# A scan layer and a spectral layer on one core: z projected at its silu, a second stream of early transforms, and a reordered second block

## The chip, the core and the metric

The kernel runs on one core of a Trainium2 chip, as one program. The metric is the device time of an execution in microseconds (us). Five engines work side by side, each through its own list of instructions in order: PE (matrix products, written to PSUM), DVE, ACT and POOL (elementwise work; only DVE and ACT touch PSUM here), and SP, which here only issues DMAs. An instruction that waits holds back all that stands behind it in its engine's list.

## The reference, cut to what matters

Layer 0 takes four images x of 128 channels by 128 x 128 pixels; an image is a sequence of 16,384 steps. Matrices are applied per step; the state has 256 x 16 entries and runs along the sequence.

```
xm = relu(x @ w1 + b1) @ w2 + b2
x_in, z = split(xm @ in_proj)
u = silu(conv4(x_in) + cb)                # 4 taps along the sequence
dt, B, C = split(u @ x_proj);  delta = softplus(dt @ dt_proj + b)
h = h * exp(delta * A) + delta * B * u    # per step: 256 x 16
y = (sum_s h * C + u * D) * silu(z)
x1 = x + silu(groupnorm(y @ out_proj))
```

Layer 1 takes x1. Per image it forms four softmax weights (from a group norm, a matrix product, a relu and a mean over pixels). Per channel it takes the 2-D Fourier transform X, and with four filters W_f returns `irfft2(X * X * sum_f weight_f * W_f) + 0.5 * x1`.

## The kernel before, in words

**Block 0 (layer 0).** The sequence is cut into 128 chunks of 512 steps, 32 per image. A chunk has 16 slots; a slot n is a pair of tiles of 128 (state, channel) rows by 512 steps. The scan runs on DVE (`scans`, L396 to L420): two scan instructions per slot (L412). In even slots POOL multiplies both results by C (L419). In odd slots DVE does that itself (L414), save for one product in some chunks that changes sides. The first tile of every even slot takes its input b from PSUM: PE transposes it there (`dbu_turn`, L375 to L383, four transposes of `bt`, which ACT makes at L304). That PSUM tile exists once. The other tiles take their input from POOL (`dbu`, L363). ACT makes the factors exp(delta A) (L393). PE sums the products over states (`sums`, L422 to L435).

The order is written out by hand. `pre(k)` and `post(k)` (L184, L437) return steps as (slot, phase, function); they are laid into a table (L505 to L548) and played slot by slot. Within a slot the phases are: turn, sums, pe, exps, late, act, pool, dbu, early, gate, scans, dve, end (L550 to L554). So in PE's list the transposes that a slot's "turn" issues come ahead of that slot's sums, and these ahead of its "pe" steps. The transposes for an even slot stand at the head of the odd slot before it. `pre(k)` runs one chunk ahead of its scan. Its steps that matter here, with the slots of a chunk counted 0 to 15:

- `cv_mm(0)`, `cv_mm(1)` (L230): the convolution, eight PE passes each, in slots 0 and 1; `silu_act` (L236) on ACT in slot 2;
- `z_mm` (L219): the z projection, in slot 14; `z_act` (L225) copies it from PSUM in slot 15; `z_silu` (L241) works in place in slot 2 of the next chunk;
- the products `h1`, `xm`, `dt` and `o` share a PSUM pool with these, the pool `pp` of two banks; `turn_bank` (L178) is one more bank, used by `xd` in slot 3, by two sets of transposes in slots 5 to 14, and by some `agg` products in slot 15.

Work of layer 1 that needs x1 of earlier images is laid into chunks of later images: `finish` (L608) with its normalisation, in chunks 2 to 18 of the next image, and with its aggregation after that. `spectrum` (L468) makes the forward transform of three (or two) channel images: load in slot 4, transform over rows in 12 (PE), copy by ACT at the end of 12, transform over columns in 13 (PE), copy by ACT and store at the end of 13. One stream of these runs from chunk 52 to the end (L528 to L538), for images 0 and 1: 25 of the 64 units of block 1 are early, that is, their transforms stand ready.

**Block 1 (layer 1).** A unit is eight channels of one image (L779 to L785); it takes three steps t. It loads x1 (`xt`, six buffers) and for an early unit its transform (`sx`, two buffers) (`load`, L807). A unit that is not early is transformed by PE, with a copy by ACT and one product by DVE (L845 to L878). ACT scales the four filters (`term`, L817), POOL adds them (`mix`, L825) and forms two sums (L894); then come products on DVE, a way back through PE, copies and a store. Filters (`ft`, four buffers) are loaded four units ahead (`loads`, L795 to L800). In the first units image 3 is still normalised (32 blocks, two per three steps), and then aggregated (one block per step, t from 70); their loads are in SP's list too, three steps ahead of use. SP loads one unit ahead (L944).

## Time and profile before

| | |
|---|---|
| time, median of 3 | 7172.46 us (7171.05 to 7173.44) |
| profiled execution | 7175.45 us, its span 7173.6 us |
| block 0 | from 0 to some 6405 us |
| block 1 | from some 6425 us to the end |
| busy in the span | DVE 96%, POOL 96%, ACT 86%, PE 82% |
| scans, L412 | 3968 of 128 x 512 with a carried state, 1255 to 1268 ns each |
| a chunk of block 0 without normalisation | 48.4 and 49.1 us in turn |
| a chunk with normalisation | 50.3 us |
| mean granted PE clock | 0.897 |

A row of a group names line, engine, operation, what is written from what, and shapes; then come the count, the engine's busy time in us, the mean duration in ns, and the idle time of the engine before such instructions with what ended it. The timeline lists start and duration. A row of the waits gives total us, times and the longest. A row of a stretch gives its length, the busy time and count of each engine, the granted PE clock (PEclk, 1.00 is full speed), the DMA share and GB/s.

### The profile page before, as it was taken

What the parts mean: (1) busy time and instruction counts of PE and PEld (TensorE: products, weight loads), DVE (VectorE), ACT (ScalarE), POOL (GpSimd) and SP (SyncE); (2) the same over time, 40 slices, a digit from 0 to 9 for tenths busy, and PEclk for the clock granted to TensorE, in tenths of its full rate; (3) what the DMA queues carried; (4) which work ended last, traced back from release to release, by engine and by line L of the source; (5) the groups of instructions that cost most, each with busy time, mean ns of one, the idle gap of its engine ahead of it and who ended that gap; (6) DMA issues with size and microseconds to landing.
All of it is one profiled execution on the core that took longest, in us unless ns stands there. A gap on an engine that the chain in (4) does not pass through costs nothing.

```text
span 7173.6 us, 91384 instructions
## 1 busy us (share of the span) xinstructions
PE 5904.2 (82%) x26708; PEld 2626.8 (37%) x26708; DVE 6892.9 (96%) x7966; ACT 6143.9 (86%) x13658; POOL 6892.5 (96%) x3188
## 2 busy tenths in 40 slices
PE   6888888788787788888888788888887888867998
PEld 2333333233222233333333333333333333326888
DVE  6999999999999999999999999999999999989777
ACT  6888888888888888888888888898888888878876
POOL 6999999999999999999999999999999999988887
PEclk8888888888888889998989899999898899979999
DMA  5666666666777777777777777777777777769866
GB/s 139 160 160 152 163 159 151 165 159 165 191 176 192 179 171 176 172 184 175 189 196 186 188 176 175 178 177 184 189 191 194 177 179 177 172 164 306 236 185 162
DMA packets 905480, 1286.20 MB, mean 179 GB/s; under 512 B 81672, under 2 KB 356752, under 8 KB 904976
## 3 DMA queue, kind: packets, MB, share of 16 engines
q1 hardware_dynamic: 904832, 1280.09, 71.9%
q8 instruction: 210, 3.44, 0.2%
q14 instruction: 294, 2.41, 0.1%
q10 hardware_dynamic: 144, 0.26, 0.0%
HBM read 1023.45 MB, written 256.58 MB: 178 GB/s over the span
## 4 chain that ended last, share of the span: by engine, by line
DVE 41%; ACT 29%; issue 11%; PE 10%; DMA 5%; POOL 3%; SPq 1%; DVEq 0%; ACTq 0%; POOLq 0%
DVE da L412 20%; DVE h L412 12%; ACT da L393 12%; DVE hb L414 5%; ACT L393 3%; DMA rdelta<-dd 2%; ACT L275 2%; ACT delta L275 2%; ACT bt L304 2%; POOL hb L363 2%; DVE zs L443 1%; PE y L433 1%; POOL hb L419 1%; ACT L242 1%; DMA xt<-x 1%
## 5 line engine op out<-in xcount | busy, mean ns | idle before, releaser
L363 POOL TENSOR_TENSOR hb<-rdu,rB 128x1536 f32<-128x1536 f32 (+2 forms) x1536 | 3605.7, 2364 | 22.4 <-DMA rdelta<-dd 21.3
L393 ACT ACTIVATE da<-rdelta,amat 128x512 f32<-128x512 f32 x4096 | 2794.1, 700 | 138.3 <-DVE h L412 133.9
L419 POOL TENSOR_TENSOR hb<-h,rC 128x1024 f32<-128x1024 f32 (+1 forms) x1072 | 2435.0, 2274 | 88.8 <-DVE h L412 73.4
L412 DVE TENSOR_TENSOR_SCAN da<-da,st,hb 128x512 f32<-128x512 f32 x1976 | 2419.8, 1267 | 21.5 <-ACT da L393 14.3
L433 PE MATMUL y<-hb,sel 128*32 128x512 f32 x8192 | 1313.4, 717 | 2.9 <-POOL hb L419 2.7
L414 DVE TENSOR_TENSOR hb<-da,rC 128x512 f32<-128x512 f32 x2040 | 1296.1, 674 | 3.0
L412 DVE TENSOR_TENSOR_SCAN h<-da,st,b 128x512 f32<-128x512 f32 x992 | 1258.3, 1268 | 1.7 <-PE b L383 1.6
L412 DVE TENSOR_TENSOR_SCAN h<-da,st,hb 128x512 f32<-128x512 f32 x1000 | 1251.6, 1255 | 1.8 <-ACT da L393 1.8
L383 PE MATMUL b<-ident,bt 128*128 128x128 f32 x4096 | 748.4, 305 | 516.1 <-DVE h L412 390.6
L234 PE MATMUL pp_cv<-xm,wck 128*128 128x512 f32 x2048 | 1014.3, 640 | 1.6 <-ACT xm L217 0.8
L304 ACT ACTIVATE bt<-pt_dut,xdt 128x256 f32<-128x256 f32 x2048 | 839.4, 474 | 184.5 <-PE pt_dut L293 184.3
L383 PEld LDWEIGHTS b<-ident,bt 128*128 128x128 f32 x4096 | 531.3, 154 | 1017.1 <-DVE h L412 692.8
L415 ACT COPY st<-da 128x1 f32<-128x1 f32 x2040 | 273.1, 160 | 474.2 <-DVE hb L414 471.1
L234 PEld LDWEIGHTS pp_cv<-xm,wck 128*128 128x128 f32 x2048 | 395.9, 204 | 651.0 <-issue 422.1
L828 POOL TENSOR_TENSOR wb<-wb,term 128x1040 f32<-128x1040 f32 x192 | 461.0, 2401 | 70.8 <-ACT term L822 62.9
L293 PE MATMUL pt_dut<-ident,du 128*128 128x128 f32 x1024 | 232.4, 338 | 285.1 <-ACT xdt L286 174.9
L429 PE MATMUL y<-u,diag 128*128 128x512 f32 x512 | 303.0, 675 | 188.7 <-DVE zs L443 187.3
L293 PEld LDWEIGHTS pt_dut<-ident,du 128*128 128x128 f32 x1024 | 132.2, 162 | 604.8 <-POOL du L312 475.9
L393 ACT ACT_TABLE_LOAD x262 | 336.1, 1283 | 12.1 <-DMA rdelta<-dd 7.4
L312 POOL TENSOR_TENSOR du<-delta,u 128x512 f32<-128x512 f32 x256 | 318.8, 1267 | 25.8 <-ACT delta L275 25.8
L223 PE MATMUL pp_z<-xm,win 128*128 128x512 f32 x512 | 274.5, 634 | 51.8 <-ACT fq L497 46.2
L267 PE MATMUL pp_dt<-xd,wdt 8*128 8x512 f32 x512 | 284.8, 642 | 33.0 <-ACT pp_o L457 23.5
(160 smaller groups left out, 8139.8 us busy)
## 6 DMA issues: line engine op xcount, KB each, us to landing
rdelta<-dd SPq DMA_DIRECT2D x1024, 256.0 KB, 4.7
rdu<-dd SPq DMA_DIRECT2D x1024, 256.0 KB, 7.5
rC<-bc SPq DMA_DIRECT2D x512, 256.0 KB, 7.3
rB<-bc SPq DMA_DIRECT2D x512, 192.0 KB, 4.7
dd<-delta SPq DMA_DIRECT2D x256, 256.0 KB, 7.2
dd<-du SPq DMA_DIRECT2D x256, 256.0 KB, 5.7
ft<-in_filt_w SPq DMA_DIRECT2D x104, 520.0 KB, 7.0
ob<-o SPq DMA_DIRECT2D x128, 256.0 KB, 2.1
```

The lines of the kernel that those rows point to most:

```text
L234: nc.tensor.matmul(ps["cv", j], w, d["xm"][:, t : t + T], start=t == 0, stop=t == KC - 1)
L293: nc.tensor.transpose(ps["dut"][:, 2 * t + j, :], d["du"][:, j, at : at + P], s.ident)
L304: nc.scalar.activation(d["bt"][:, 2 * h + t, :, q, :], src, AF.Copy, scale=d["xdt"][:, 2 * h + t, R + q : R + q + 1])
L312: nc.gpsimd.tensor_tensor(du, d["delta"][:, j, :], d["u"][:, j, :], ALU.mult)
L363: nc.gpsimd.tensor_tensor(hb[:, p : p + n, :], d["du", j][:, m : m + n, :], d["B"][:, p - 1 : p - 1 + n, :], ALU.mult)
L383: nc.tensor.transpose(b[:, t * P : (t + 1) * P], src, s.ident)
L393: nc.scalar.activation(da, d["delta", j][:, m, :], AF.Exp, scale=s.amat[:, c : c + 1])
L412: nc.vector.tensor_tensor_scan(o, das[q], b, init, ALU.mult, ALU.add)
L414: nc.vector.tensor_tensor(hb[:, p + q, :], das[q], d["C"][:, p + q, :], ALU.mult)
L419: nc.gpsimd.tensor_tensor(hb[:, ps, :], h[:, q, :], d["C"][:, ps, :], ALU.mult)
L433: nc.tensor.matmul(y[m * DG : (m + 1) * DG, :], s.sel, d["hb", j, r][:, p, :], start=False, stop=r == NG - 1)
L828: nc.gpsimd.tensor_tensor(wb, wb, u[n].terms[f], ALU.add)
```

## The change

In block 0, z is no longer copied. Its first half is projected in slot 1 of the next chunk into `turn_bank`; its second half is projected from within `silu_act` in slot 2, as soon as the silu of the first convolution half has freed a bank. The silu then reads PSUM, one half at a time. The convolution moves one slot forward, to slots 15 and 0. A second stream of `spectrum` runs from chunk 84 one slot behind the first (slots 13 and 14); both take channels from the highest down. 39 units are early: all of images 0 and 1, and seven of image 2. A stream holds one SBUF tile for load, copy and store.

In block 1 the late units of image 3 stand one by one between those of images 0, 2 and 1, where before they stood in runs. A filter is kept if its next use is up to two units on. SP loads a unit two ahead, in the middle step of a unit. Units 27 to 38 are now all early; of units 42 to 60 nine are, mostly every other one. By the code the filters for units 49 and 56 are now loaded one step ahead of their use, and unit 63 loads filters once more.

```diff
-            def z_mm():
-                for j in range(NH):
-                    ps["z", j] = psum(f"z_{k}_{j}")
-                    w = s.win[:, DI + j * P : DI + (j + 1) * P]
-                    nc.tensor.matmul(ps["z", j], w, d["xm"][:, HALO:], start=True, stop=True)
-
-            def z_act():
-                d["zs"] = p2.tile([P, NH, T], F32, tag="zs", name=f"zs_{k}")
-                for j in range(NH):
-                    nc.scalar.copy(d["zs"][:, j, :], ps["z", j])
+            def z_mm(j, home):
+                ps["z", j] = home(f"z_{k}_{j}")
+                w = s.win[:, DI + j * P : DI + (j + 1) * P]
+                nc.tensor.matmul(ps["z", j], w, d["xm"][:, HALO:], start=True, stop=True)
...
                 for j in range(NH):
                     nc.scalar.activation(u[:, j, :], ps["cv", j], AF.Silu, bias=s.cb[:, j : j + 1])
+                    if j == 0 and k:
+                        st[k - 1]["z"](1, psum)
+                if k:
+                    st[k - 1]["z silu"]()
 
             def z_silu():
-                nc.scalar.activation(d["zs"], d["zs"], AF.Silu)
+                d["zs"] = p2.tile([P, NH, T], F32, tag="zs", name=f"zs_{k}")
+                for j in range(NH):
+                    nc.scalar.activation(d["zs"][:, j, :], ps["z", j], AF.Silu)
...
-                (0, "pe", partial(cv_mm, 0)), (1, "pe", partial(cv_mm, 1)), (2, "act", silu_act),
-                (NP - 2, "pe", z_mm), (NP - 1, "act", z_act), (NP + 2, "act", z_silu), (3, "pe", xd_mm), (4, "act", xd_act), (5, "pe", dt_mm), (5, "pe", xd_turn),
+                (-1, "pe", partial(cv_mm, 0)), (0, "pe", partial(cv_mm, 1)), (2, "act", silu_act),
+                (NP + 1, "pe", partial(z_mm, 0, turn_bank)), *([(NP + 2, "act", z_last)] if k == B * NCH - 1 else []), (3, "pe", xd_mm), (4, "act", xd_act), (5, "pe", dt_mm), (5, "pe", xd_turn),
...
-            return [
-                (4, "pe", load), (12, "pe", over_h), (12, "end", evict), (13, "pe", over_w), (13, "end", store),
-            ]
+            return list(zip(*zip(*slots), (load, over_h, evict, over_w, store)))
...
+        ways = [
+            ((4, "pe"), (12, "pe"), (12, "end"), (13, "pe"), (13, "end")),
+            ((5, "pe"), (13, "pe"), (13, "end"), (14, "pe"), (14, "end")),
+        ]
+        ready = [(b + 1) * NCH + NCH // 2 + 4 for b in range(B - 1)]
+        images = [(b, c0) for b in range(B - 1) for c0 in reversed(range(0, C, CC))]
+        queues = [images, [x for x in images if x[0]]]
+        free = [ready[0], ready[1]]
...
         for n, c0 in enumerate(rest):
-            units += [(c0, b) for b in (0, 2, 1, 3)]
-            for c1 in late[n * len(late) // len(rest) : (n + 1) * len(late) // len(rest)]:
-                units.append((c1, B - 1))
+            full = [(c1, B - 1) for c1 in late[n * len(late) // len(rest) : (n + 1) * len(late) // len(rest)] + [c0]]
+            for b in (0, 2, 1):
+                units += [(c0, b)] + full[:1]
+                full = full[1:]
+            units += full
...
-            ft = next((x for x in spans if x.c0 == c0 and (n - x.last == 1 or (c0 in kept and b == B - 1))), None)
+            ft = next((x for x in spans if x.c0 == c0 and (n - x.last <= 2 or (c0 in kept and b == B - 1))), None)
...
             load(0)
+            load(1)
             for t in range(3 * N + LAG + 3):
                 n, i = divmod(t, 3)
                 if i == 0:
                     for ft in loads[n]:
                         load_filter(ft)
-                    load(n + 1)
...
                 elif i == 1:
+                    load(n + 2)
                     term(n + 1, 0)
```

More of the change, by code (lines that the diff above doesn't have):

```diff
@@ L39 @@
 CC = 8
-EARLY = 2
 KEEP = 4
@@ L148 @@
     stats, outs, spectra = {}, {}, set()
-    spec = [dpool.tile([H, C, 2, WF], F32, tag=f"spec_{b}", name=f"spec_{b}") for b in range(EARLY)]
+    spec = [dpool.tile([H, C, 2, WF], F32, tag=f"spec_{b}", name=f"spec_{b}") for b in range(B - 1)]
     shared = SimpleNamespace(**{k: v for k, v in locals().items() if k not in ("ctx", "tc")})
@@ L239, in silu_act, with z_last @@
                     nc.scalar.activation(u[:, j, :], ps["cv", j], AF.Silu, bias=s.cb[:, j : j + 1])
+                    if j == 0 and k:
+                        st[k - 1]["z"](1, psum)
+                if k:
+                    st[k - 1]["z silu"]()
             def z_silu():
-                nc.scalar.activation(d["zs"], d["zs"], AF.Silu)
+                d["zs"] = p2.tile([P, NH, T], F32, tag="zs", name=f"zs_{k}")
+                for j in range(NH):
+                    nc.scalar.activation(d["zs"][:, j, :], ps["z", j], AF.Silu)
+            def z_last():
+                z_mm(1, psum)
+                z_silu()
+            d["z"], d["z silu"] = z_mm, z_silu
             def xd_mm():
@@ L466, in post, with spectrum @@
             ]
-        def spectrum(b, c0, n):
+        def spectrum(b, c0, n, way, slots):
             g = {}
             def load():
-                g["x"] = p1.tile([s.H, 3, s.W], F32, tag="fx", name=f"fx_{b}_{c0}")
-                nc.sync.dma_start(out=g["x"][:, 0:n], in_=s.x1[b][c0 : c0 + n].rearrange("c h w -> h c w"))
+                g["x"] = p1.tile([P, 3, 2 * s.WF], F32, tag=f"fs{way}", name=f"fs_{b}_{c0}")
+                nc.sync.dma_start(
+                    out=g["x"][:, 0:n, 0 : s.W], in_=s.x1[b][c0 : c0 + n].rearrange("c h w -> h c w")
+                )
@@ L476, in over_h @@
             def over_h():
-                g["pa"] = psp.tile([s.W, 3, 2 * s.WF], F32, tag="pp", name=f"pp_fa_{b}_{c0}")
+                ps = g["ps"] = psp.tile([P, 3, 2 * s.WF], F32, tag="pp", name=f"pp_fa_{b}_{c0}")
                 for q in range(n):
-                    nc.tensor.matmul(g["pa"][:, q], g["x"][:, q], s.fh, start=True, stop=True)
+                    nc.tensor.matmul(ps[:, q], g["x"][:, q, 0 : s.W], s.fh, start=True, stop=True)
             def evict():
-                g["sa"] = p1.tile([s.W, 3, 2 * s.WF], F32, tag="fs", name=f"fs_{b}_{c0}")
@@ L483, in evict @@
-                nc.scalar.copy(g["sa"][:, 0:n], g["pa"][:, 0:n])
+                nc.scalar.copy(g["x"][:, 0:n], g["ps"][:, 0:n])
             def over_w():
                 half = s.H // 2
-                g["px"] = psp.tile([s.H, 3, 2 * s.WF], F32, tag="pp", name=f"pp_fx_{b}_{c0}")
+                ps = g["ps"] = psp.tile([P, 3, 2 * s.WF], F32, tag="pp", name=f"pp_fx_{b}_{c0}")
                 for q in range(n):
-                    re, im = g["sa"][:, q, 0 : s.WF], g["sa"][:, q, s.WF :]
+                    re, im = g["x"][:, q, 0 : s.WF], g["x"][:, q, s.WF :]
@@ L490, in over_w @@
                     for (data, a, b_), start in (((re, s.fwr, s.fwr), True), ((im, s.fwi, s.fwm), False)):
                         for at, w in ((0, a), (1, b_)):
-                            o = g["px"][at * half : (at + 1) * half, q]
+                            o = ps[at * half : (at + 1) * half, q]
                             nc.tensor.matmul(o, data[:, at : at + half], w, start=start, stop=not start)
             def store():
-                x = p1.tile([s.H, 3, 2, s.WF], F32, tag="fq", name=f"fq_{b}_{c0}")
@@ L497, in store @@
-                nc.scalar.copy(x[:, 0:n].rearrange("h c r k -> h c (r k)"), g["px"][:, 0:n])
-                nc.sync.dma_start(out=s.spec[b][:, c0 : c0 + n], in_=x[:, 0:n])
-            return [
-                (4, "pe", load), (12, "pe", over_h), (12, "end", evict), (13, "pe", over_w), (13, "end", store),
-            ]
+                evict()
+                o = s.spec[b][:, c0 : c0 + n].rearrange("h c r k -> h c (r k)")
+                nc.sync.dma_start(out=o, in_=g["x"][:, 0:n])
+            return list(zip(*zip(*slots), (load, over_h, evict, over_w, store)))
@@ L527, in block0 @@
                 todo[at + (b + 1) * NCH * NP, phase].append(f)
-        chunk = NCH + NCH // 2 + 4
-        for b in range(EARLY):
-            for c0 in range(0, C, CC):
-                chunk = max(chunk, (b + 1) * NCH + NCH // 2 + 4)
-                if chunk + 3 > n_chunks:
-                    break
-                for at, n in ((0, 3), (3, 3), (6, 2)):
-                    for slot, phase, f in spectrum(b, c0 + at, n):
-                        todo[slot + chunk * NP, phase].append(f)
-                    chunk += 1
-                s.spectra.add((c0, b))
+        ways = [
[6 more added lines that the diff above has]
+        free = [ready[0], ready[1]]
+        while True:
+            way = min((0, 1), key=lambda w: free[w])
+            group = next((x for x in queues[way] if x[::-1] not in s.spectra), None)
+            if group is None:
+                break
+            b, c0 = group
+            chunk = max(free[way], ready[b])
+            if chunk + 3 > n_chunks:
+                break
+            for at, n in ((0, 3), (3, 3), (6, 2)):
+                for slot, phase, f in spectrum(b, c0 + at, n, way, ways[way]):
+                    todo[slot + chunk * NP, phase].append(f)
+                chunk += 1
+            free[way] = chunk
+            s.spectra.add((c0, b))
         for n in range(n_chunks * NP):
```

## The prediction

> **What bounds the kernel now.** I read the page's busy lines and slices, then two stretches, then what DVE waits for, then the timeline of one chunk.

> ```profile
> PE 5904.2 (82%) x26708; PEld 2626.8 (37%) x26708; DVE 6892.9 (96%) x7966; ACT 6143.9 (86%) x13658; POOL 6892.5 (96%) x3188
> ...
> DVE  6999999999999999999999999999999999989777
> ...
> POOL 6999999999999999999999999999999999988887
> ```
> ```profile
> 90.00:6405.00 6315.00, 5213.18 (x21533) 2003.58 (x21531) 6284.67 (x6578) 5510.87 (x12364) 6235.77 (x2848) 0.89 0.72 175
> 6425.00:7173.60 748.60, 631.61 (x5020) 599.87 (x5020) 573.40 (x1340) 584.89 (x1199) 620.98 (x320) 0.95 0.79 225
> ```
> Columns: PE, PEld, DVE, ACT, POOL busy, then the PE clock. In block 0 DVE is idle 6315 - 6285 = 30 us of 6315: nothing in block 0 can be worth more than 30 us unless DVE itself gets less to do, and the change takes no DVE instruction from block 0. Each stall that it adds to DVE there counts in full. In block 1 no engine is full.

> ```profile
> DVE sa L860 <- ACT sa L853: 114.9, 82, 5.8
> DVE h L412 <- PE b L383: 40.0, 4, 38.4
> ```
> The second row is the one to watch: DVE waited for the transposed input b four times, 38.4 us of it at the start. So b is never late now. How near is it? A chunk without spectra, PE, from the end of slot 14:

> ```profile
> 2175.10 0.55 PE L383 MATMUL b<-ident,bt 128*128 128x128 f32 x3 [1.88 <-DVE h L412]
> 2176.52 0.33 PE L383 MATMUL b<-ident,bt 128*128 128x128 f32 x1 [0.87 <-ACT bt L304]
> 2176.78 1.15 PE L433 MATMUL y<-hb,sel 128*32 128x512 f32 x8
> 2177.86 5.27 PE L234 MATMUL pp_cv<-xm,wck 128*128 128x512 f32 x8
> 2182.96 0.60 PE L383 MATMUL b<-ident,bt 128*128 128x128 f32 x4
> 2183.49 1.06 PE L433 MATMUL y<-hb,sel 128*32 128x512 f32 x8
> ```
> and DVE's scan of slot 2, which reads that last b:
> ```profile
> 2185.57 1.27 DVE L412 TENSOR_TENSOR_SCAN h<-da,st,b 128x512 f32<-128x512 f32 x1
> ```
> b is ready at 2183.56, 2.0 us early. The first rows show what ties PE to DVE: the b for slot 0 waits for a scan and for ACT's bt, so the convolution cannot start earlier than it does. This first half took 5.27 us; a later one in the same chunk takes 3.70. The stretches of 3.41 us, on whose grid the granted clock changes in the trace, say why:
> ```profile
> 2174.22:2177.63 3.41, 1.66 (x12) 0.60 (x12) 3.41 (x4) 3.41 (x10) 3.41 (x3) 1.00 0.35 101
> 2177.63:2181.04 3.41, 3.41 (x8) 1.50 (x5) 3.41 (x5) 2.54 (x7) 3.41 (x2) 0.50 1.07 222
> ```
> PE was busy 1.66 of 3.41 us, and the next stretch was granted half the clock. Counted over the whole trace: all 98 full-clock stretches with PE under 40% busy were followed by half clock, 23 of 40 between 40 and 50%, 112 of 1524 above. Back to full took a stretch over 90% busy (198 of 204), at 80 to 90% half of the time, below never.

> **Part 1: the convolution in slots 15 and 0.** In the new order PE does: b for slot 0, sums, convolution half 0, half 1, b for slot 2. Half 1 (8 passes at 0.43 = 3.44 us) is moved ahead of the transposes for slot 2. In the chunk above: 2182.96 + 3.44 + 0.60 = 2187.0 against 2185.57, so DVE stalls 1.4 us. With a full clock, another chunk: convolution from 504.63, + 3.54 + 3.44 + 0.60 = 512.21 against a scan at 512.52: no stall, 0.3 to spare. A chunk with one stream: 5265.32 + 7.58 = 5272.90 against 5272.73: 0.2 us. The edge is thin and the clock decides. I did this sum for every chunk with its own rows: with the clocks as before 1.64 us a chunk for chunks 1 to 32, 1.41 for 34 to 49, 1.25 for 52 to 64, 0.35 for 66 to 81 and 98 to 113, 0.4 to 0.6 for the rest: some 124 us. With every convolution pass at full speed from where it starts today the same sum gives 54, and about 25 if the sums before it run at full speed too, as at 503.63.

> **Part 2: z leaves slot 14.** The two z products (2.14 us of PE a chunk) filled the time before the b of slot 0. Without them PE in the chunk above has nothing from 2171.24 to 2175.10, and again 0.87 us: on any position of the grid one stretch is under about 43% busy. So without a stream nearly every chunk gets half clock, where today 9 of 48 escape. It lasts until a full stretch of work has passed, 2.0 to 5.4 us after 2176.5, and costs half of that, 1.0 to 2.7; less 0.3 to spare this is 0.7 to 2.4 us. The chunks that throttle today come to 1.2 to 2.9. I take 1.7 for 50 chunks: **85 us**. With one stream (chunks 52 to 83) its column transform ends at 5260.26 in the chunk quoted, the b starts at 5262.62 and waits 0.96: idle 2.1 + 1.0 us, under 45% for some 70% of the positions. A throttled chunk loses 0.2 + 1.5 to 2.9, one that is not 0.2. I take 1.2 for 32: **38 us**.

> [...]

> On ACT the copy goes (2 x 615 ns, L228) and a silu of 1057 becomes two; the nearest row is u's, from PSUM, 674 each. That is 0.94 us less a chunk, 120 us in all, and worth nothing: DVE is the bound. The second z product waits for u's first silu and stands ahead of the b for slot 4. At 0.5 to 1.0 us late it is still some 2 us early for DVE, because in slot 2 PE has only 1.1 us of z and sums otherwise. If that cover went, each chunk would lose up to 1 us (128 us); I take 0.

> **Part 3: second stream**, 14 more units, 42 groups. PE: 0.83 + 1.48 us a group (L479, L493); ACT 2 copies of 0.37 to 0.50; loads and stores of 14 x 1.05 MB over 2185 us, 7 GB/s on 178. PE is then busy in slots 13 and 14, so these 44 chunks keep their clock. But the copy at the end of slot 13 stands in ACT's list ahead of the bt that the b of slot 0 waits for: 0.2 (above) + 0.4, less ACT's slack of up to 0.4 where there is some. I take 0.5 for 44: **22 us**; bounds 0.1 and 2.3 (a whole group's PE time on the path).

> Block 0: 85 + 38 + 22 = 145, less some 5 of today's 30 us of waits (z behind the spectra's copies): **+140**. Bounds +25 (full clock) and +230.

> **Part 4: block 1.** A unit that is not early has 96 PE passes at 0.111 us = 10.7 us; early 48, 5.4. POOL has 3 x 2.40 (L828) + 2 x 1.30 (L899, L900) = 9.8 us for every unit. Now units 36 to 63 take 7157.4 - 6843.7 = 313.7 us between their last products, 11.6 each: PE's 10.7, and three waits of some 6 us (PE for xt, behind four filter issues) that loads two ahead remove. After, PE's mean over these 27 is 8.5 and POOL is late next: 27 x 9.8 = 265, + 8 for waits, + 2 x 6 where filters for units 49 and 56 are issued one step (3.3 us) ahead, with 7.0 us to land: 285, **-29**. In units 24 to 36 (133 us) POOL's floor would give -6 to -17, but units 27 to 38 are all early on two sx buffers: the load of unit n+2 waits on SP for the products of unit n, three steps on, and the aggregation's loads (needed then) stand behind it on SP. Some 7 us to land, 6 times, half hidden: +6 to +20. I take 0. Units 0 to 24 keep their pattern of early units, at a DMA share of 0.95: 0. Block 1: **-30**, bounds -66 and +10.

> **Sum**, on the profiled execution: 7175.45 + 140 - 30 = 7285; that execution is 3 us above the median of the runs, so 7282.

> **Rivals.** (a) The clock holds: PE finds work in slots 13 and 14, or half clock falls elsewhere. Then block 0 costs 25 - 5, block 1 gives 30 to 66: 7175 + 20 - 45 = 7150, faster. For it: at full clock b has 0.3 us to spare. Against it: 98 of 98. It decides if fewer than about 15 chunks throttle before slot 2. (b) The lateness is real but small, as in the full-clock sum (54): 7175 + 54 - 5 - 50 = 7174, no change. (c) The second stream piles up: ACT's copies and the banks put 2.3 us, not 0.5, on each of 44 chunks: 7285 + 79 = 7364. The bound of +10 in block 1 would add 40 to any.

> **Numbers.** 0.2% is 14 us, about what a measurement of this kernel tells from no change. Forecast (7215 to 7340) 0.70; (a) 0.12, mostly faster; (b) 0.10, of it 0.07 within 0.2% and 0.03 slower; (c) 0.08. Faster 0.12, same 0.07, slower 0.81. The range takes (b)'s edge and not (a) or (c): 7165 to 7345.

> **What would show it.** Right: DVE's wait "h L412 <- PE b" grows from 40 us to over 120, once a chunk, at slot 2; the two convolution halves stand back to back ahead of b; half clock in slots 15 to 0 of nearly all chunks up to 51; chunks there of 50 us for 48.7; block 1 near 720 us with POOL over 90% busy from unit 36. Wrong: that wait stays under 50 us, chunks still take 48.4 and 49.1, or the chunks from 84 lose more than those before 50.

## The result, and the profile after

The changed kernel takes **7410.11 us** (median of 4 runs, 7407.16 to 7413.45), against 7171.76 us for the kernel before, run beside it: a ratio of 1.0333, with a 95% interval from 1.0315 to 1.035. It is slower by 238 us; the forecast was 110 slower, with a range that ended at 7345. The direction and the named wait were right. The size was wrong by more than a factor of two.

The profiled execution of the changed kernel has a span of 7405.4 us. Its page, the busy lines and slices that answer to those of before:

```profile
PE 5965.3 (81%) x27156; PEld 2671.2 (36%) x27156; DVE 6886.0 (93%) x7924; ACT 6071.4 (82%) x13572; POOL 6896.6 (93%) x3188
...
DVE  6999999999999999989999999999999999997878
...
POOL 6999999999999999988999999998999999997988
```

DVE did nearly the same work (6886 us for 6893) in a longer span. The stretches of the two blocks, in the columns named in the prediction:

```profile
90.00:6689.00 6599.00, 5344.66 (x22652) 2128.25 (x22650) 6299.37 (x6578) 5458.29 (x12320) 6241.12 (x2848) 0.87 0.69 169
6710.00:7405.40 695.40, 560.28 (x4348) 519.42 (x4348) 551.43 (x1298) 565.12 (x1157) 619.46 (x320) 0.95 0.89 256
```

Block 0: DVE is now idle 6599 - 6299 = 300 us, where it was idle 30. Block 1 is shorter, and PE has 4348 products there for 5020. Taken at the start of the last slot's scan, block 0 grew from 6406.3 to 6690.4 us (**+284**) and the rest fell from 767.2 to 715.0 (**-52**). What DVE waits for:

```profile
DVE h L417 <- PE b L388: 246.9, 121, 37.4
DVE da L417 <- ACT da L398: 56.5, 29, 5.8
DVE sa L878 <- ACT sa L871: 48.4, 35, 3.5
```

The first row was 40.0 us in 4 waits, and is now 121 waits. The third belongs to block 1; it was 114.9 us in 82 waits. The second, for the factors from ACT, was this before:

```profile
DVE da L412 <- ACT da L393: 14.3, 8, 2.9
```

The prediction has no word on it. One chunk shows the first row. PE in the timeline at the start of chunk 43 of the changed kernel, the place that the prediction shows from before (start, us, what, idle time before it and what ended it):

```profile
2274.00 0.90 PE L388 MATMUL b<-ident,bt 128*128 128x128 f32 x3 [3.80 <-DVE h L417]
2275.42 0.47 PE L388 MATMUL b<-ident,bt 128*128 128x128 f32 x1 [0.52 <-ACT bt L309]
2275.82 1.94 PE L438 MATMUL y<-hb,sel 128*32 128x512 f32 x8
2277.69 8.17 PE L227 MATMUL pp_cv<-xm,wck 128*128 128x512 f32 x16
2285.70 0.60 PE L388 MATMUL b<-ident,bt 128*128 128x128 f32 x4
```

and DVE's scan of slot 2 in the same timeline:

```profile
2286.33 1.28 DVE L417 TENSOR_TENSOR_SCAN h<-da,st,b 128x512 f32<-128x512 f32 x1 [1.78 <-PE b L388]
```

PE has nothing for 3.80 us, then does the sums in 1.94 us at a granted clock of 0.50 (1.06 at full clock, as in the rows before), then 16 convolution passes in one row, where 8 stood before, and only then b. DVE waits 1.78 us for it.

Where block 0's 284 us are, by the lengths of chunks (from the first scan of slot 0 to the next), each kernel of the experiments against the kernel before, in us:

| | chunks 1 to 51, no stream | 52 to 59, 65 to 83, one stream | 13 chunks with `agg` in slot 15 | 84 to 91, 97 to 123, two streams | block 0 | block 1 |
|---|---|---|---|---|---|---|
| forecast | 85 | 38 (with five `agg` chunks) | 0 of its own | 22 (with eight) | +140 | -30 |
| **after** | **120.5** | **65.4** | **69.0** | **28.6** | **+284** | **-52** |
| e1 convolution back | 45.5 | 27.9 | 15.4 | 3.9 | +98 | -54 |
| e2 convolution moved alone | 110.6 | 10.4 | 40.5 | 12.5 | +176 | -2 |
| e3 fill | 44.8 | 15.6 | 59.7 | 33.1 | +155 | -55 |
| e5 `agg` ahead | 119.7 | 65.1 | 29.3 | 29.7 | +244 | -52 |
| e7 one stream | 119.8 | 65.4 | 72.0 | 85.3 | +344 | -43 |
| e9 z and convolution as before | 0.6 | -0.1 | 2.2 | 0.3 | +2 | -50 |
| e10 e1, z behind convolution | 22.6 | 28.1 | 15.3 | 4.1 | +72 | -54 |
| e11 fill and `agg` | 33.3 | 11.9 | 18.9 | 32.4 | +97 | -56 |
| e16 e10 with fill | 7.0 | 4.3 | 9.9 | 4.8 | +28 | -55 |

The columns are named for the changed kernel; e2 and e7 have one stream in chunks 84 to 123 too. The 13 chunks are 60 to 64, 92 to 96 and 124 to 126. In chunks 1 to 51 of the changed kernel 119.6 of the 120.5 us were lost between the scans of slots 1 and 2, where DVE waits for b. The table is from profiled executions; the medians stand below.

### The profile page after: what moved, and what is told of

The parts are those of the page before. It is cut to its first block, busy times and chain, and to the rows that moved or that the text cites. A ratio compares the mean times of both kernels' runs of the same rounds, so it can differ in the third digit from the quotient of the medians.

```text
span 7405.4 us, 92571 instructions
## 1 busy us (share of the span) xinstructions
PE 5965.3 (81%) x27156; PEld 2671.2 (36%) x27156; DVE 6886.0 (93%) x7924; ACT 6071.4 (82%) x13572; POOL 6896.6 (93%) x3188
## 4 chain that ended last, share of the span: by engine, by line
DVE 35%; ACT 25%; PE 18%; issue 9%; POOL 6%; DMA 5%; SPq 1%; DVEq 0%; ACTq 0%; POOLq 0%
DVE da L417 15%; ACT da L398 10%; DVE h L417 10%; PE pp_cv L227 8%; DVE hb L419 4%; PE y L438 3%; POOL hb L368 3%; ACT bt L309 3%; POOL hb L424 2%; ACT L398 2%; ACT L280 2%; ACT delta L280 2%; DVE zs L448 2%; PE y L434 1%; DVE pr L910 1%
## 5 line engine op out<-in xcount | busy, mean ns | idle before, releaser
L438 PE MATMUL y<-hb,sel 128*32 128x512 f32 x8192 | 1348.0, 735 | 3.1 <-POOL hb L424 2.7
L227 PE MATMUL pp_cv<-xm,wck 128*128 128x512 f32 x2048 | 1036.9, 663 | 1.8 <-ACT bv L671 1.1
L227 PEld LDWEIGHTS pp_cv<-xm,wck 128*128 128x128 f32 x2048 | 426.9, 215 | 677.1 <-issue 672.0
L198 PE MATMUL pp_h<-xt,w 128*128 128x512 f32 x512 | 307.2, 729 | 7.8 <-DMA xt<-in_x 4.3
L438 PEld LDWEIGHTS y<-hb,sel 128*32 128x32 f32 x8192 | 173.3, 116 | 374.2 <-issue 278.5
```

The lines of the kernel that those rows point to most:

```text
L227: nc.tensor.matmul(ps["cv", j], w, d["xm"][:, t : t + T], start=t == 0, stop=t == KC - 1)
L438: nc.tensor.matmul(y[m * DG : (m + 1) * DG, :], s.sel, d["hb", j, r][:, p, :], start=False, stop=r == NG - 1)
```

## The experiments

**e1: the convolution back.** The changed kernel with

```diff
-                (-1, "pe", partial(cv_mm, 0)), (0, "pe", partial(cv_mm, 1)),
+                (0, "pe", partial(cv_mm, 0)), (1, "pe", partial(cv_mm, 1)),
```

> The changed kernel with one thing undone: the convolution halves stand in slots 0 and 1 again, z stays at its silu, the second stream and the second block stay. Theory (the loss is convolution half 1 standing ahead of the transposes for slot 2, and the aggregation product standing behind half 0): block 0 comes back to within 40 us of the 6406 us of before, block 1 keeps its 52 us, so 7120 to 7160 us, faster than both kernels; DVE's wait for b falls from 247 us to under 90. Rival (the loss is the PE idle that z left behind, or the second stream, wherever the convolution stands): most of the 284 us stay, 7300 us or more.

Measured: 7218.35 us, ratio to before 1.0063 (1.0048 to 1.0078); DVE's wait for b fell to 43.4 us in 8 waits. The time lies between the two theories. Putting the convolution back takes 186 of the 284 us away, but 98 stay with z and the streams alone. 78 of them are lost between the scans of slots 3 and 5, where DVE now waits for ACT more often than before:

```profile
DVE da L417 <- ACT da L398: 32.8, 53, 3.3
DVE h L417 <- ACT da L398: 21.0, 27, 1.3
```

**e2: the convolution moved alone.** The kernel before with that line reversed, and z's copy at the head of slot 15.

> The kernel before with one thing done: the convolution halves stand in slots 15 and 0; z stays in slot 14 and its copy is issued at the head of slot 15, so that its banks are free. Theory: with the clocks as in the kernel before my chunk by chunk sum gave 124 us, and the aggregation product behind convolution half 0 adds 50 to 65 that I had left out: 7172 + 180 = 7350 us (7300 to 7390). Rival (the order alone is nearly harmless, the half clock that comes when z leaves slot 14 makes the loss): under 7240 us.

Measured: 7347.02 us, 1.0242 (1.0227 to 1.0258). The sum is as the theory said, but its columns don't agree with the parts of the prediction: up to chunk 51 the loss is 110.6 us with z still in slot 14, nearly the 120.5 of the changed kernel. In the one-stream chunks it is 10.4 for 65.4.

**e3: PE's idle time filled.** The changed kernel with

```diff
+            def fill():
+                if 0 < k < FILL:
+                    for n in range(3 if k < 52 else 2):
+                        t = psum(f"fill_{k}_{n}")
+                        nc.tensor.matmul(t, s.win[:, DI : DI + P], d["xm"][:, HALO:], start=True, stop=True)
...
+                (NP - 2, "pe", fill),
```

> The changed kernel with three more products of z's shape in slot 14 of chunks 1 to 51 and two in chunks 52 to 83, whose results nobody reads: only PE's idle time ahead of b for slot 0 is filled. Theory (the half clock makes the stall large): PE then keeps its full clock through the convolution, the 2.3 us lost a chunk up to 51 and the 2.6 us up to 83 fall under 0.7 us, which is 100 to 150 us less: 7260 to 7310 us, although PE has 213 products more. Rival (the order alone makes the stall, the clock hardly matters): 7390 to 7430 us, the same chunks still lose over 2 us.

Measured: 7271.83 us, 1.0134 (1.0117 to 1.0151): 138 us less with more work. In the chunks without a stream and with one, the loss fell from 186 us to 60 (0.88 and 0.58 us a chunk, where I expected under 0.7), so the half clock after PE's idle time makes two thirds of the loss there. Of block 0's 284 us it makes 129. Half clock (mean under 0.9 over the first 3.4 us of convolution half 0) fell on 51 of chunks 1 to 51 in the changed kernel, 49 in e2, 27 here and 42 before; of chunks 65 to 83 on 19, none, 1 and 1. Two stretches of the changed kernel at the start of chunk 70, a one-stream chunk, and PE's two idle times there:

```profile
3696.34:3699.75 3.41, 1.29 (x12) 0.61 (x12) 3.41 (x4) 3.41 (x10) 3.41 (x3) 1.00 0.60 175
3699.75:3703.17 3.42, 3.42 (x11) 1.18 (x4) 3.42 (x5) 1.85 (x5) 3.42 (x2) 0.50 1.03 259
```
```profile
3697.31 0.55 PE L388 MATMUL b<-ident,bt 128*128 128x128 f32 x3 [2.49 <-DVE h L417]
3699.01 0.33 PE L388 MATMUL b<-ident,bt 128*128 128x128 f32 x1 [1.15 <-ACT bt L309]
```

PE is busy 1.29 of 3.41 us, the next stretch is granted 0.50, and it is the stretch of the convolution. All 19 such stretches of chunks 65 to 83 followed one with PE 0 to 42% busy (a single one of them with PE idle throughout). The two idle times in this chunk, 2.49 and 1.15 us, are both shorter than a stretch of 3.41.

**e4: the second block alone**, in the kernel before. **e6: of that, only the loads two ahead:**

```diff
             load(0)
+            load(1)
...
-                    load(n + 1)
...
                 elif i == 1:
+                    load(n + 2)
```

> The kernel before with the changed second block alone (alternating units, filters kept over two units, loads two ahead), and 25 early units as before, so no second stream. Theory: a unit that is not early still costs PE 10.7 us, so from unit 36 only the three waits of 6 us go, and of the 52 us that block 1 gained some 20 come back: 7150 us (7140 to 7165). Rival (the order and the loads two ahead are the whole gain, the 14 units more in the second stream give nothing): 7120 to 7130 us.

> The kernel before with one thing done: the second block loads a unit two ahead, in the middle step; order of the units and early units as before. Theory: PE's waits for xt in units 36 to 63 go (three of some 6 us) and the rest of the 41 us that the second block alone gave belongs to the order: 7150 to 7158 us. Rival a (the loads are the whole gain): 7135 us. Rival b (the order is the whole gain): 7168 us or more.

Measured: e4 7132.16 us, 0.9944 (0.9929 to 0.9959); e6 7132.57 us, 0.9945 (0.993 to 0.996). Both of my theories fell, and e6's rival (a) held. The loads alone give all of the 41 us, and the order, with 25 early units, nothing: from unit 36 the two kernels agree unit by unit. A unit's time is counted here from the last instruction of the unit before to its own (DVE's, ahead of the store). Units 43, 50 and 57 go from 16.5, 16.9 and 18.8 us to 10.6 each, and 40, 47 and 54 from 13.3, 12.9 and 12.7 to 9.4, in all 31 us; units 1 to 24 give 7. From unit 36 PE is then the limit; a stretch of e6 has it busy 280 of 285 us:

```profile
6830.00:7115.00 285.00, 280.15 (x2475) 277.74 (x2474) 235.74 (x570) 233.81 (x484) 263.09 (x136) 1.00 0.75 202
```

**e5: the aggregation product ahead of the sums** of slot 15 (its phase "sums" for "pe"), in the changed kernel. The reason stands in the timeline of chunk 61 of the changed kernel. PE:

```profile
3265.60 5.71 PE L227 MATMUL pp_cv<-xm,wck 128*128 128x512 f32 x8
3271.14 1.02 PE L679 MATMUL pt_agg<-x,weff 128*128 128x512 f32 x2
```

ACT, which reads that product and then makes factors:

```profile
3272.26 0.66 ACT L683 ACTIVATE pt_agg<-pt_agg,bv 128x512 f32<-128x512 f32 x1 [8.30 <-PE pt_agg L679]
...
3272.94 0.71 ACT L398 ACTIVATE da<-rdelta,amat 128x512 f32<-128x512 f32 x1
```

and DVE's next scan:

```profile
3274.46 2.47 DVE L417 TENSOR_TENSOR_SCAN da<-da,st,hb 128x512 f32<-128x512 f32 x2 [5.84 <-ACT da L398]
```

The product stands behind convolution half 0, ACT stands 8.30 us for it, and the factors behind that on ACT come 5.84 us late.

> The changed kernel with the aggregation product of slot 15 issued ahead of that slot's sums, and so ahead of convolution half 0 on PE. Theory (in chunks 60 to 64, 92 to 96 and 124 to 126 the product waits behind half 0, ACT waits for it, and the next factors stand behind on ACT): these 13 chunks, which lose 69 us in all against before, fall to the rate of their neighbours, some 18 us, plus up to 1 us each because the product now delays the convolution: 40 to 50 us less than the changed kernel, 7360 to 7370 us. Rival (the product's place doesn't matter, it is only one more thing that PE must do before b): within 15 us of the changed kernel, 7395 us or more.

Measured: 7367.75 us, 1.0274 (1.0257 to 1.0291), 42 us less; the 13 chunks fell from 69.0 to 29.3 us. As expected.

**e7: one stream**, the changed kernel with `way = 0`.

> The changed kernel without the second stream: 25 early units from one stream as before. Theory (work for PE in slots 13 and 14 keeps the clock): chunks 84 to 126, which lose 67 us with two streams, lose like chunks 65 to 83, 2.6 us each, so 35 to 50 us more in the first block, and 12 us more in the second: 7450 to 7475 us, slower than the changed kernel although PE and ACT do less. Rival (the second stream costs the 22 us that I forecast): 7390 to 7405 us.

Measured: 7474.83 us, 1.0422 (1.0407 to 1.0438). In the changed kernel the second stream is worth 65 us: it is work for PE in slots 13 and 14, and chunks 97 to 123 lose 0.6 us each with it, 2.5 without. Half clock at convolution half 0 fell on 1 of these 27 chunks with it, and on all 27 without.

**e8, e9: the second stream and second block beside z and a convolution that stay where they were**, the second stream's last two steps in slot 15 and z's copy at the head of slot 15, as in e2:

```diff
-            ((5, "pe"), (13, "pe"), (13, "end"), (14, "pe"), (14, "end")),
+            ((5, "pe"), (13, "pe"), (13, "end"), (15, "pe"), (15, "end")),
```

> The second stream and the changed second block without the moves of z and of the convolution: both stand where they stood before, z is copied, and the second stream's column transform is put into slot 15, behind the transposes for slot 0. Theory: block 0 loses under 15 us, since b for slot 2 is 2 us early, and the second block takes 713 us as in the changed kernel, 12 less than with 25 early units: 7118 to 7135 us, the fastest of all. Rival (two streams pile up on the two banks and on ACT whatever else is done): 7150 us or more.

> The same kernel as in the last run with the second stream beside an unmoved z and convolution, again, for a trace that can be read and a narrower interval. Theory, mended: its 7130 us is 2 us under the kernel with the second block alone, so block 0 should have lost some 10 us in chunks 84 to 126 (0.2 us each, more in the chunks with an aggregation product) and the second block gained 12. Rival: block 0 lost nothing and the 14 further early units bring nothing in the second block.

Measured: 7129.85 us, and the second time 7130.68, 0.9941 (0.9928 to 0.9953); the split is from the second. Block 0 lost 2 us, not 10. Units 36 to 63 take 255.6 us against 268.1 in e4, but units 24 to 36 take 139.4 against 133.9: the gain of 14 more early units is 12 us there, of which 5 are given back, and the whole can't be told from e4.

**e10: z's first half behind the convolution half** in slot 1 of e1 (phase "exps" for "pe").

> The kernel with the convolution back in slots 0 and 1, with one exchange more: z's first half stands behind convolution half 1 in slot 1, not ahead of it. Theory (with the convolution back, what is left is ACT: its silu of convolution half 1 waits for PE, then two silus of z and a table load stand ahead of the factors for slot 4): half 1 ends 1.0 us earlier, the 0.7 us a chunk in slot 4 and the 1.1 us in the chunks with normalisation go for the most part: 40 to 60 us less than 7218, 7160 to 7180 us. Rival (the silus are late because of their own length and z's second half, which ends no earlier): 7210 us or more.

Measured: 7196.13 us, 1.0032 (1.002 to 1.0044): 22 us less, half of what was expected. So the place of z's first product ahead of half 1 made 26 of the 98 us that block 0 lost in e1, and 72 stay.

**e11: both mendings**, e5 with four filling products and three in one-stream chunks.

> The changed kernel with both mendings at once: unread products in slot 14 (four in chunks 1 to 51, three in chunks 52 to 83) and the aggregation product ahead of the sums. Theory (the first block's 284 us are the clock, some 155, the aggregation product, some 42, and the order at full clock, 30 to 50, with two streams 30 to 40): 7410 - 155 - 42 = 7213 us, 7195 to 7230, and half clock at convolution half 0 in fewer than 10 of chunks 1 to 51. Rival (the two shares overlap, or four products delay b for slot 0 themselves): 7250 us or more.

Measured: 7218.58 us, 1.0064 (1.005 to 1.0077). The time is as expected, and the shares add. But half clock still fell on 18 of chunks 1 to 51, where I expected fewer than 10, and chunks 1 to 31 lose 0.70 us each with four products and lost 0.74 with three. A price that hardly moves with the work pointed to the next three.

**e13, e14, e15: one product more, one less, two more** on the path, in the changed kernel; e13:

```diff
+                if j:
+                    for _ in range(1):
+                        nc.tensor.matmul(ps["cv", j], s.wck[:, 0, P:], d["xm"][:, 0:T], start=True, stop=True)
                 for t in range(KC):
```

e15 has two of them; e14 has `[0, 2, 3]` as the taps of half 1, so it leaves out one tap of the convolution.

> The changed kernel with one product more in every chunk, the convolution's first tap of half 1 made twice (0.87 us of PE at full clock), ahead of the transposes for slot 2. Lock theory: a stretch of half clock begins and ends on the grid of 3.41 us, so PE work that starts d later in it ends only d/2 later, and a chunk settles where its length is a whole number of stretches; two chunks then take 30 of them (102.4 us) and 0.87 us more of work moves the phase and not the length. Chunks 1 to 31 keep 102.4 us a pair (or jump to 31 stretches, 105.8, but nothing between), while chunks 97 to 123, at full clock, lose 0.8 us each more: 7430 to 7460 us. Linear theory (each stall is the work that is late, and 30.0 is chance): 104.1 us a pair, 0.87 us in nearly every chunk, 7500 to 7520 us.

> The changed kernel with one product less in every chunk: the second tap of convolution half 1 is left out (a part of the computation is missing). Lock theory: chunks 1 to 31 take 30 stretches of 3.41 us a pair as before (102.4 us), or fall to 29 (99.0), nothing between; chunks 97 to 123 win their 0.6 us. Linear theory: 100.6 us a pair, 0.87 us less in every chunk that stalls.

> The changed kernel with two products more ahead of the transposes for slot 2, 1.74 us of PE at full clock in every chunk. Lock theory: 102.4 or 105.8 us a pair in chunks 1 to 31, nothing between; chunks 97 to 123 lose 1.7 us each more. Linear theory: 105.9 us a pair, which doesn't tell the two apart by itself, but then the run with one product more lies half way, and in the lock theory it does not.

Measured, mean length of two chunks in a row in chunks 6 to 31, in us and in stretches of the clock's grid:

| | us | a pair, us | stretches of 3.4133 us |
|---|---|---|---|
| before | 7171.76 | 97.49 | 28.56 |
| after | 7410.11 | 102.40 | 30.00 |
| e2 | 7347.02 | 102.40 | 30.00 |
| e13, one more | 7470.98 (1.0409, 1.0379 to 1.044) | 102.40 | 30.00 |
| e14, one less | 7301.09 (1.0173, 1.0143 to 1.0202) | 98.99 | 29.00 |
| e15, two more | 7591.05 (1.0577, 1.0546 to 1.0607) | 104.96 | 30.75 |
| e3, e11, fill | 7271.83, 7218.58 | 99.03, 98.93 | 29.01, 28.98 |

Two stretches of 102.40 us, one after the other, of the changed kernel:

```profile
1000.00:1102.40 102.40, 80.98 (x308) 30.69 (x304) 97.64 (x102) 82.79 (x186) 96.77 (x45) 0.83 0.63 151
1102.40:1204.80 102.40, 80.97 (x308) 30.70 (x304) 97.64 (x102) 82.81 (x186) 96.72 (x45) 0.83 0.64 151
```

and of e13:

```profile
1000.00:1102.40 102.40, 81.59 (x309) 30.88 (x308) 97.64 (x102) 82.77 (x186) 96.77 (x44) 0.83 0.63 151
1102.40:1204.80 102.40, 81.60 (x309) 30.87 (x308) 97.64 (x102) 82.78 (x186) 96.78 (x44) 0.83 0.63 150
```

DVE is busy 97.64 us of 102.40 in all four. A product more in each chunk cost these chunks nothing: in chunks 1 to 31 e13 lost 0.4 us in all. The start of a chunk moved on the grid instead, from 1.2 to 2.9 us after a stretch begins, 1.7 = 2 x 0.87, as the lock theory has it. In chunks 97 to 123 (half clock on 1 of these 27 in the changed kernel) the same product cost 1.14 us each (0.8 expected; 2.27 for two, 1.7 expected; one less saved 0.3, 0.6 expected). That, with 1 us in each of chunks 32 to 59, makes e13 slower than the 7460 I allowed. e15 shows that the lock is looser than I said: no single pair of chunks keeps a whole number; four pairs together take 123 stretches. In chunks 35 to 48 e15 takes 16.00 stretches a chunk and e1 15.00, and from chunk 40 to 49 the changed kernel takes 46.00 in three chunks. The rows e3 and e11 are near 29 and not locked: most pairs take 98.92 and 98.93 us (28.98), so the start of a chunk slides on the grid by some 0.06 us a pair.

**e16: e10 with filling products** (three and two, as in e3).

> The kernel with the convolution back in slots 0 and 1 and z's first half behind it, with three unread products in slot 14 of chunks 1 to 51 and two in chunks 52 to 83. Clock theory (what z at its silu still costs, 72 us of the first block, is half clock after the idle time that z left): with the clock kept the convolution ends 1 to 2 us earlier, ACT's silus no longer wait, the first block comes back to within 20 us of 6406 us, 7125 to 7145 us in all. Rival (the cost is ACT's list: two silus of z and a table load stand ahead of the factors for slot 4 whatever the clock): 40 us or more of the 72 stay, 7160 us or more.

Measured: 7145.58 us, 0.9964 (0.9952 to 0.9975). Of e10's 72 us in block 0, 44 go and 28 stay, a little more than the 20 that I expected. Half clock fell on 34 of chunks 1 to 51, for all 51 in e10. So the half clock is the larger part of what z at its silu costs there. The silus of z in ACT's list can be the rest; this is not shown.

**e12: sx one unit ahead, x1 two**, in e9:

```diff
                     load(n + 2)
+                    load_spectrum(n + 1)
```

> The fastest kernel so far (second stream, z and convolution as before, second block as changed) with one thing more: a unit's transform sx is loaded one unit ahead instead of two, while x1 stays two ahead. Theory (with loads two ahead SP stands 73 us before the sx buffer is free, with the aggregation's loads behind it, and units 27 and 30 take 17.6 and 17.9 us for 11.4): units 24 to 36 fall from 149 us (unit 23's end to 36's) to 130 to 138, the whole to 7113 to 7122 us. Rival (the sx then lands too late for ACT, 9.8 us after its issue being too little beside the filters): 7130 us or more.

What SP's own queue waited for between 6725 and 6870 us at the sx load (line, released by, us, times, longest), in e9:

```profile
SPq L827 <- DVE sq L898: 72.9, 9, 10.8
```

and in e12:

```profile
SPq L831 <- DVE sq L902: 31.9, 9, 6.9
```

Measured: 7126.09 us, 0.9936 (0.9923 to 0.995). Units 27 and 30 fell from 17.6 and 17.9 us to 9.4, units 24 to 36 from 139.4 to 115.1: the place where the loads two ahead do harm is shown. But units 0 to 24 took 9.7 us more and units 36 to 63 8.6 us more (why is not shown; sx may be needed sooner there), and the whole is 5 us better, less than the intervals and outside the 7113 to 7122 expected. e6, one small edit, and e12 both are faster than the kernel before, by 40 and 47 us against the runs beside them.

## Why the prediction was wrong

**Parts 1 and 2, chunks without a stream: mechanism right, size and cause wrong.** 85 us forecast for 50 chunks, 120.5 measured in 51. The step that failed is the sum "with the clocks as before", chunk by chunk with its own rows. With the stalls the clocks didn't stay as before: half clock fell on 51 chunks instead of 42, and pairs of chunks settled at 30.0 stretches. From 97.49 to 102.40 is 2.46 us a chunk, where I took 1.7 (and 1.64 for the moved convolution without the idle time). That a stalled chunk is held on the clock's grid is what e13 and e14 show, with 30.00 and 29.00 stretches a pair. I made z's leaving slot 14 the cause. It does bring half clock to every chunk (51 of 51 in e1), but it adds little here: the moved convolution alone loses 110.6 us (e2), z's move without it 45.5 (e1), both together 120.5. The parts don't add.

**Part 2, one-stream chunks: 1.2 us each forecast, 2.4 measured** (65.4 us in 27 chunks). Here z's leaving is the cause: 10.4 us with z in place, 15.6 with the idle time filled. The 70% of positions on the grid was too low: 24 of the 27 were throttled, 19 of 19 in chunks 65 to 83.

**Left out: the aggregation product.** It moved from ahead of the convolution to behind half 0 and had no term in the sum: PE, then ACT's wait for it, then the factors behind that on ACT. 69.0 us in 13 chunks, 40 of it from the product's place (e5).

**z at its silu: taken at 0**, because b for slot 4 was "still some 2 us early". Alone it isn't free: with the convolution back (e1) block 0 keeps 98 us, and e9, which differs from e1 in z's place (and in where the second stream ends), 2. Most of it is half clock (e16) and the product's place on PE (e10). In chunks 1 to 51 of the changed kernel nothing is lost between the scans of slots 3 and 5 (42 us in e1); DVE has waited for b at slot 2 by then.

**Part 3, the second stream: cost near, worth wrong.** 0.5 us a chunk forecast, 0.8 measured in 35 chunks (28.6). That it keeps the clock was right (e7: half clock on 1 of chunks 97 to 123 with it, on all 27 without). But I compared it with chunks as they were before; without it these chunks lose 85.3 us (e7), so here it saves 57. How much of the 28.6 us are ACT's copies, as the forecast had it, was not separated, so the near number is partly luck. Rival (c) didn't happen.

**Part 4: -30 forecast, -52 measured.** Right: PE's waits for xt, and POOL as the next limit. POOL is busy 273.5 of 285 us here:

```profile
7110.00:7395.00 285.00, 259.28 (x2178) 250.45 (x2179) 235.57 (x570) 230.78 (x476) 273.54 (x143) 0.99 0.85 231
```

Counted as in the forecast, between the last products on DVE, units 36 to 63 took 264.4 us, for 313.7 before and 285 forecast. That is POOL's 27 x 9.8 us alone: the 12 us for late filters and 8 for waits didn't come. Units 0 to 24 gave 9 us, forecast 0. Units 24 to 36 lost 6, taken as 0, with the sx wait where I put it.

Of the signs that I had listed, one long wait at slot 2, halves back to back, half clock in all chunks up to 51 and block 1 at 715 us came; the chunks took 51.2 us, not 50. Rivals (a) and (b) needed a clock that holds, and fell with the half clock in all 51 chunks.

## What to carry to other kernels

When a change makes a steady loop late on an engine whose granted clock follows how busy it was, as PE's did here (in the kernel before, all 98 full-clock stretches with PE under 40% busy were followed by half clock), don't add up stalls with the clocks of the old trace. The loop can settle on the clock's grid, as chunks 1 to 31 did here, and then the price goes in steps (30.00 stretches a pair in e13, 29.00 in e14), so a sum is only a first guess beside the whole multiples near it. Before steps are taken out of an idle place or moved ahead, ask what their work kept alive there, and go through everything that they now precede in that engine's list and what other engines stand behind it. Try the parts of a large change alone: one small edit (loads one unit earlier) held 41 of the second block's 52 us, while the rest of the change, taken together, made the kernel slower.
